# A router's way between token-major and expert-major: TensorE transposes against VectorE 32x32 transposes and a DRAM copy

## The chip, the cores and the metric

One core of a Trainium2 chip runs the whole kernel. The metric is the device time of one execution in microseconds; the figure quoted for a kernel is the median of its runs. Engines are named as in the profile: PE is TensorE's matmul, PEld its weight load, DVE is VectorE, ACT is ScalarE, POOL is GpSimd, SP is the sync engine, which here only issues DMAs.

## What is computed

Four conditional layers are added to a residual stream x of shape (8, 256, 1024), all in float32. Cut to what matters:

```python
# L0: dense layer plus a mixture of 8 low-rank experts, top 2 by logits
logits = x @ Wr.T + 5 * one_hot(language_id, 8)        # (8, 256, 8)
topw, topi = top_k(logits, 2)
gates = sum(one_hot(topi) * softmax(topw))             # (8, 256, 8)
h = einsum('btd,erd->bter', x, A)                      # rank 16 for each expert
x = x + x @ W.T + 2 * einsum('bter,bte,eor->bto', h, gates, B)
# L1: dense, bias, and a per-batch signed mask
x = x + x @ W1.T + b + coeff[b] * (x @ (2 * mask[b] - 1))
# L2: one dense matrix per batch, chosen by an id;  L3: rank 16, chosen by the same id
x = x + x @ w2[id[b]].T
x = x + (x @ B3[id[b]].T) @ A3[id[b]].T
```

The change touches only how `logits` and `gates` are brought from one layout to another.

## The kernel before, in words

Activations are held feature-major: 128 features on the partitions, tokens along the free dimension. Two batches make a pair of 512 tokens, and two pairs make a half `g` (0 or 1). A half goes through L0, and then each of its two pairs through L1, L2 and L3. Every large product is made of three float32r matmuls, from a rounded high part and a low part of each operand. ACT makes the high parts (`highs`, line 285), DVE the low parts by subtraction (`lows`, line 291). The high parts have five buffers and the low parts four, so an engine that prepares operands can be only about two slots ahead of PE.

L0 of a half runs in 16 **slots** (`l0_slot`, line 816). It uses seven products of a Strassen scheme over quadrants of W (named A) and of x (named B); differences such as S1, S4, T1, T3 are made in place, partly by accumulating DMAs from the POOL queue (`add`, line 699). The work around a product is written out by hand: `l0_works` (line 690) lists for each slot what DVE, ACT, POOL and SP are given before the product, in list order, after that slot's high and low parts; a negative slot number means before them. `l0_mids` (line 777) lists what PE is given in the middle of a slot's product or, for a negative number, after it. Each engine and each DMA queue works through what it was given in order.

**The router.** For a pair p, `logits(p)` (line 301) makes eight matmuls of 32 weight columns (8 of them used) by 512 tokens. They are spread over the four 32-column groups of the array, two contraction blocks on each, so PSUM then holds four partial sums on partition groups 0, 32, 64 and 96. ACT copies this bank to SBUF (`leave`, line 310). `by_token(p)` (line 315) makes four TensorE transposes, so that tokens lie on the partitions. `router` (line 323) adds the four partial sums with a DVE reduction, adds the language bias and finds the two best experts in 12 more small DVE operations. `weigh` (line 358) takes an exponential on ACT and makes the gates on DVE. `expand(p)` (line 378) repeats each gate 16 times, once for each rank, with a DVE copy. `gates_by_rank(p)` (line 387) makes four more TensorE transposes and an ACT copy into `gts[p]`: 128 partitions (expert, rank) by 512 tokens. `gate(p)` (line 405) multiplies this by the experts' products `phs[p]` on DVE; `split_gates` (line 398) makes the high part on ACT (`ghi`) and the low part on DVE (`glo`). PE uses these in `lora` (line 647): at the end of slot 5 for the first pair p0 of a half, in slot 9 for the second pair p1, in slots 13 and 15 again.

In half 0, p0 is pair 1 and p1 is pair 0. The logits of p0 are made in `head` (line 848), those of p1 in the middle of slot 3. In half 1 both pairs' logits are made near the end of the previous pair's L2 (line 932), and `router` and `weigh` run once for both (line 999).

**SP's queue.** At the start SP issues all loads that half 0 of L0 needs (lines 1066 to 1087), ending with the two halves of quadrant A22. What follows in its queue is `load_unit` (line 214), which is called from slot 7 on and loads a mask block (line 225), and for some units a block of W1 (line 222). The pool for these blocks has nine buffers, and the eight quadrants of W fill eight of them. Stores of results go through the same queue (line 474).

Of the kernel before, what the change touches and what calls it, by code (L numbers as in the profile page):

```python
# [8 lines left out]
F32 = mybir.dt.float32  # L9
# [3 lines left out]
ALU = mybir.AluOpType  # L13
AX = mybir.AxisListType

P = 128
NB = 8
T = 256
N = 2 * T
K = 8  # L20
E = 8
R = 16
# [12 lines left out]
def kernel(ctx: ExitStack, tc: tile.TileContext, x, lang, coeff, ids,  # L35
# [14 lines left out]
    nc = tc.nc  # L50
# [8 lines left out]
    gp = ctx.enter_context(tc.tile_pool(name="g", bufs=1))  # L59
    ps = ctx.enter_context(tc.tile_pool(name="ps", bufs=2, space=PS))  # L60
    aux = ctx.enter_context(tc.tile_pool(name="aux", bufs=1, space=PS))

    f32 = lambda ap: ap.bitcast(F32)
    mm = nc.tensor.matmul
# [2 lines left out]
    def tt(o, a, b, op):  # L67
        nc.vector.tensor_tensor(o, a, b, op)  # L68

    def bank(n, name):  # L70
        return aux.tile([P, N], F32, tag=f"ax{n}", name=name)
# [30 lines left out]
    c_sb = cst.tile([P, NB], F32, name="c_sb")  # L102
    ids_raw = cst.tile([1, NB], I32, name="ids_raw")
    b1_sb = cst.tile([P, K], F32, name="b1_sb")
    bias = cst.tile([P, NB, E], F32, name="bias")
    c2 = cst.tile([P, NB], F32, name="c2")
    negc = cst.tile([P, NB], F32, name="negc")
    ids_sb = cst.tile([1, NB], I32, name="ids_sb")
# [8 lines left out]
    def constants():  # L117

        lang_f = cst.tile([P, NB], F32, name="lang_f")
        nc.vector.tensor_scalar(lang_f, lang_i, -1.0, float(E), ALU.mult, ALU.add)  # L120
        tt(bias, rev.to_broadcast([P, NB, E]),
           lang_f.rearrange("p (b o) -> p b o", o=1).to_broadcast([P, NB, E]), ALU.is_equal)
        nc.vector.tensor_scalar(bias, bias, 5.0, None, ALU.mult)
        nc.vector.tensor_scalar(c2, c_sb, 2.0, None, ALU.mult)
        nc.vector.tensor_scalar(negc, c_sb, -1.0, None, ALU.mult)

        neg = cst.tile([1, NB], F32, name="neg")
        idf = cst.tile([1, NB], F32, name="idf")
        nc.vector.tensor_scalar(neg, ids_raw, 0.0, float(E), ALU.is_lt, ALU.mult)
        tt(idf, ids_raw, neg, ALU.add)  # L130
        nc.vector.tensor_scalar(ids_sb, idf, 0.0, float(E - 1), ALU.max, ALU.min)
# [164 lines left out]
        ready["lo"] = max(ready["lo"], n + 1)  # L296


    lgs, pts = {}, {}

    def logits(p):


        g, j = p // 2, 1 - p % 2
        pl = bank(j, f"pl{p}")
        for k in range(K):
            c = 32 * (k % 4)
            mm(pl[c:c + 32, :], wrs[:, k, :], X[g][:, j, k, :], start=(k < 4), stop=(k >= 4))  # L308

        def leave():  # L310
            lgs[p] = gp.tile([P, N], F32, tag="lg", name=f"lg{p}", bufs=3)
            copy(lgs[p], pl)
        return leave

    def by_token(p):
        pts[p] = bank(1 - p % 2, f"pt{p}")
        lg = lgs.pop(p)
        for n in range(4):
            nc.tensor.transpose(pts[p][:, n * P:(n + 1) * P], lg[:, n * P:(n + 1) * P], ident)  # L319

    gxs, routed = {}, {}

    def router(pairs):
        n4 = 4 * len(pairs)
        t = lambda nm, w: gp.tile([P, n4, w], F32, tag=nm, name=nm)
        lv = t("lv", E)
        for i, p in enumerate(pairs):
            quarters = pts.pop(p).rearrange("p (n g e) -> p n e g", n=4, g=4)[:, :, :E, :]
            nc.vector.tensor_reduce(
                lv[:, 4 * i:4 * i + 4].rearrange("p n (e o) -> p n e o", o=1), quarters, AX.X,  # L330
                ALU.add)
        b0, nb = 2 * pairs[0], 2 * len(pairs)
        lv4 = lv.rearrange("p (b h) e -> p b h e", h=2)
        tt(lv4, lv4, bias[:, b0:b0 + nb].rearrange("p b (o e) -> p b o e", o=1)
           .to_broadcast([P, nb, 2, E]), ALU.add)
        revb = rev.to_broadcast([P, n4, E])

        def top(v, nm):
            mx = t(f"mx{nm}", 1)
            nc.vector.tensor_reduce(mx, v, AX.X, ALU.max)  # L340
            eq = t(f"eq{nm}", E)
            tt(eq, v, mx.to_broadcast([P, n4, E]), ALU.is_equal)
            tt(eq, eq, revb, ALU.mult)
            fi = t(f"fi{nm}", 1)
            nc.vector.tensor_reduce(fi, eq, AX.X, ALU.max)
            oh = t(f"oh{nm}", E)
            tt(oh, revb, fi.to_broadcast([P, n4, E]), ALU.is_equal)
            return mx, oh

        m1, oh1 = top(lv, "1")  # L350
        rest = t("rest", E)
        nc.vector.scalar_tensor_tensor(rest, oh1, -3.0e38, lv, ALU.mult, ALU.add)
        m2, oh2 = top(rest, "2")
        d = t("d", 1)
        tt(d, m2, m1, ALU.subtract)
        routed[tuple(pairs)] = d, oh1, oh2

    def weigh(pairs):

        n4 = 4 * len(pairs)  # L360
        t = lambda nm, w: gp.tile([P, n4, w], F32, tag=nm, name=nm)
        d, oh1, oh2 = routed.pop(tuple(pairs))
        ex = t("ex", 1)
        nc.scalar.activation(ex, d, AF.Exp)

        den = t("den", 1)
        nc.vector.tensor_scalar(den, ex, 1.0, 0.5, ALU.add, ALU.mult)
        wt1 = t("wt1", 1)
        nc.vector.reciprocal(wt1, den)
        wt2 = t("wt2", 1)  # L370
        tt(wt2, wt1, ex, ALU.mult)
        tt(oh1, oh1, wt1.to_broadcast([P, n4, E]), ALU.mult)
        tt(oh2, oh2, wt2.to_broadcast([P, n4, E]), ALU.mult)
        tt(oh1, oh1, oh2, ALU.add)
        for i, p in enumerate(pairs):
            gxs[p] = oh1[:, 4 * i:4 * i + 4, :]

    def expand(p):

        gx = gp.tile([P, 4 * E, R], F32, tag="lg", name=f"gx{p}", bufs=3)  # L380
        nc.vector.tensor_copy(gx, gxs[p].rearrange("p n (e o) -> p (n e) o", o=1)
                              .to_broadcast([P, 4 * E, R]))
        gxs[p] = gx

    gts, gates, phs = {}, {}, {}

    def gates_by_rank(p):

        pg = bank(1 - p % 2, f"pg{p}")
        gx = gxs.pop(p)  # L390
        for n in range(4):
            nc.tensor.transpose(pg[:, n * P:(n + 1) * P],  # L392
                                gx[:, n * E:(n + 1) * E, :].rearrange("p e r -> p (e r)"),
                                ident)
        gts[p] = gp.tile([P, N], F32, tag="lg", name=f"gt{p}", bufs=3)
        copy(gts[p], pg)

    def split_gates(key, gt):
        hi = gp.tile([P, N], FR, tag="ghi", name="ghi", bufs=2)
        lo = gp.tile([P, N], FR, tag="glo", name="glo", bufs=2)  # L400
        copy(hi, gt)
        tt(lo, gt, f32(hi), ALU.subtract)
        gates[key] = hi, lo
# [286 lines left out]
    def l0_works(g):  # L690
# [5 lines left out]
        def at(s, *fs):  # L696
            w.setdefault(s, []).extend(fs)
# [24 lines left out]
        def both(f, *args):  # L722
            return [lambda h=h: f(h, *args) for h in range(2)]
# [8 lines left out]
        if g == 0:  # L732
            at(1, constants, *both(s1_add))
            at(2, *both(less, "T1", 1, 0), lambda: router([p0]))
            at(3, lambda: weigh([p0]), lambda: expand(p0), lb_parts, *subs("S2", "A11", "S1"))
            at(4, *both(s4_add), lambda: gate(p0))
            at(5, lambda: router([p1]))
            at(6, lambda: weigh([p1]), lambda: expand(p1))
        else:
            at(0, *both(s1_add), *both(less, "T1", 1, 0))  # L740
            at(2, lambda: expand(p0))
            at(3, *subs("S2", "A11", "S1"))
            at(4, *both(s4_add), lambda: gate(p0))
            at(5, lambda: expand(p1))
        at(-5 if g else 4, lambda: split_gates(p0, gts[p0]))
        at(4, *both(less, "T3", 1, 1))
        t2 = subs("T2", "T1", "B22")
        at(7, t2[0], *both(s3_add))
# [28 lines left out]
    def l0_mids(g):  # L777


        p0, p1 = pair_of(g, 0), pair_of(g, 1)  # L780
        if g == 0:
            return {3: lambda: [logits(p1)(), gates_by_rank(p0)], -3: lambda: by_token(p1),
                    7: lambda: gates_by_rank(p1)}
        mids = {0: lambda: proj_pair(1, 0), 1: lambda: rank_pair(1, 1, (0, 1)),
                2: lambda: gates_by_rank(p0), 6: lambda: gates_by_rank(p1)}
        mids.update({s: lambda: fill(2) for s in (3, 4, 5, 7)})
        return mids

# [59 lines left out]
    def head():  # L848

        chain(0, 0)  # L850
        for s in range(2):
# [10 lines left out]
            for k in range(2):  # L862
# [16 lines left out]
                low(w, k, m * P, m * P + P)  # L879
                la_parts(0, m, m + 1)  # L880
                if m == 3:
                    leave = logits(1)
                    highs(4)
                    leave()
                product(s, 0, [k], start=(s == 0), order=order)
                experts(0, 1, v, m, k)
            folded.update((v, w))
        by_token(1)


    pos_tile = {}
# [7 lines left out]
    def main(n):  # L899
# [16 lines left out]
        else:  # L916
# [12 lines left out]
                    mid = [lambda: fill(2)]  # L929
            if q == 1:  # L930
                if u == 13:
                    mid = [lambda: [leave() for leave in [logits(p) for p in (2, 3)]]]
                if u == 14:
                    mid = [lambda: [by_token(p) for p in (2, 3)]]
            if q == 3:
                b = NB - 1
                if u == 9:
# [249 lines left out]
```

## Time and profile before

| | |
|---|---|
| median of 3 runs (600.59 to 601.76) | 600.69 us |
| the profiled execution | 600.37 us |
| its span in the profile | 598.5 us |
| PE busy | 590.9 us, 99% of the span |
| DVE busy / ACT busy / POOL busy | 472.7 / 386.5 / 135.7 us |
| moved by DMA | 130.22 MB, mean 218 GB/s |
| logits: matmul records | 64, of 592 ns each (median) |
| transposes: matmul records | 32, of 272 ns each (median) |

[...] successive matmuls overlap; so the price of one is read from the distance between starts, not from its duration. Each float32 matmul of the logits appears as two records, each transpose and each float32r matmul as one.

### The profile page before, as it was taken

How to read it: one execution, taken by the hardware profiler on the slowest of the kernel's cores; microseconds unless marked ns; L12 is line 12 of the kernel's file. 1: busy time of each engine (PE TensorE's matmuls, PEld its weight loads, DVE VectorE, ACT ScalarE, POOL GpSimd, SP SyncE). 2: the span in 40 equal slices, each digit the busy share in tenths (PEclk: the TensorE clock that was granted, in tenths of full speed). 3: DMA queues.
4: the chain of work that ended last, by engine and by line, in shares of the span. 5: the costliest groups of instructions: out<-in, count | busy, mean ns of one | idle time of the engine just before them, and what ended most of it. 6: DMA issues, size and time to landing. Idle time of an engine off the chain costs nothing.

```text
span 598.5 us, 8945 instructions
## 1 busy us (share of the span) xinstructions
PE 590.9 (99%) x3240; PEld 500.1 (84%) x3240; DVE 472.7 (79%) x561; ACT 386.5 (65%) x460; POOL 135.7 (23%) x178
## 2 busy tenths in 40 slices
PE   9999999999999999999999999999999999999995
PEld 7777888888888888888778888888888888888884
DVE  6678788899789998585856796789968999966863
ACT  5667566687669886544553874568866888764431
POOL 2322260113131143122110234100433110421000
PEclk9999999999999999999999999999999999999999
DMA  8987894567685777499940799836767576745704
GB/s 295 334 208 162 199 238 129 202 251 258 222 271 185 290 271 251 156 367 346 266 70 34 157 247 235 243 106 211 291 201 258 205 292 231 298 158 184 240 1 140
DMA packets 39533, 130.22 MB, mean 218 GB/s; under 512 B 4802, under 2 KB 6466, under 8 KB 38722
## 3 DMA queue, kind: packets, MB, share of 16 engines
q1 hardware_dynamic: 34594, 112.36, 53.1%
q0 software_dynamic: 4608, 16.78, 15.2%
q10 hardware_dynamic: 288, 0.52, 0.3%
q8 instruction: 25, 0.41, 0.3%
q14 instruction: 18, 0.15, 0.1%
HBM read 121.25 MB, written 8.39 MB: 217 GB/s over the span
## 4 chain that ended last, share of the span: by engine, by line
PE 97%; ACT 1%; issue 0%; DVE 0%; DVEq 0%; POOL 0%; POOLq 0%; ACTq 0%
PE po L614 59%; PE mm L614 29%; PE pl L308 1%; PE pf L470 1%; PE pb L442 1%; PE ph L645 1%; PE ph L643 1%; PE ph L644 1%; PE warm L1052 1%; ACT whi L288 1%; PE pb L493 0%; PE po L561 0%; ACT x L719 0%; PE pg L392 0%; PE pt L319 0%
## 5 line engine op out<-in xcount | busy, mean ns | idle before, releaser
L614 PE MATMUL po<-hl,whi 128*128 128x512 f32 x1016 | 244.8, 391 | 0.0
L614 PEld LDWEIGHTS po<-hl,whi 128*128 128x128 f32 x1016 | 186.0, 188 | 35.6
L68 DVE TENSOR_TENSOR wlo<-raw,whi 128x1024 fp32r<-128x1024 f32 x128 | 159.8, 1256 | 4.0 <-issue 2.0
L288 ACT CAST whi<-raw 128x1024 fp32r<-128x1024 f32 x128 | 133.7, 1048 | 18.1 <-PE mm L614 8.3
L614 PEld LDWEIGHTS po<-hl,wlo 128*128 128x128 f32 x1016 | 130.4, 191 | 7.2 <-issue 2.5
L614 PE MATMUL po<-hl,wlo 128*128 128x256 f32 x1016 | 133.4, 283 | 0.0
L614 PE MATMUL mm<-whi,whi 128*128 128x512 f32 x224 | 88.5, 395 | 0.1
L614 PE MATMUL mm<-wlo,whi 128*128 128x512 f32 x224 | 87.7, 391 | 0.0
L235 POOL TENSOR_TENSOR raw<-raw,ident 128x128 f32<-128x128 f32 x72 | 59.2, 827 | 120.8 <-DMA raw<-in_w 95.9
L257 ACT ACTIVATE raw<-raw,negc,c 128x1024 f32<-128x1024 int32 x64 | 79.6, 1243 | 4.2 <-DMA raw<-in_mask 4.0
L614 PE MATMUL mm<-whi,wlo 128*128 128x512 f32 x224 | 70.6, 390 | 0.0
L68 DVE TENSOR_TENSOR raw<-raw,w 128x1024 f32<-128x1024 f32 x56 | 69.3, 1238 | 1.2 <-issue 1.2
L235 POOL TENSOR_TENSOR w<-w,ident 128x128 f32<-128x128 f32 x28 | 32.4, 1157 | 164.2 <-DMA w<-in_w 110.7
L68 DVE TENSOR_TENSOR wlo<-x,whi 128x1024 fp32r<-128x1024 f32 (+1 forms) x38 | 44.3, 1175 | 15.6 <-issue 6.8
L587 ACT COPY c<-po 128x512 f32<-128x512 f32 (+1 forms) x34 | 18.8, 552 | 50.6 <-PE po L614 50.6
L614 PEld LDWEIGHTS mm<-whi,whi 128*128 128x128 f32 x224 | 42.3, 189 | 10.7 <-issue 1.3
L288 ACT CAST whi<-A 128x1024 fp32r<-128x1024 f32 x26 | 27.3, 1051 | 36.0 <-PE mm L614 24.0
L614 PEld LDWEIGHTS mm<-whi,wlo 128*128 128x128 f32 x224 | 42.2, 188 | 9.0
L614 PEld LDWEIGHTS mm<-wlo,whi 128*128 128x128 f32 x224 | 42.2, 188 | 8.5
L590 ACT ACTIVATE sum<-po,b_sb 128x512 f32<-128x512 f32 (+1 forms) x36 | 23.1, 640 | 30.0 <-PE po L614 30.0
L288 ACT CAST whi<-x 128x1024 fp32r<-128x1024 f32 x34 | 35.3, 1049 | 10.8 <-PE mm L614 10.7
L68 DVE TENSOR_TENSOR wlo<-A,whi 128x1024 fp32r<-128x1024 f32 (+3 forms) x37 | 35.7, 980 | 7.8 <-DMA A<-in_w 5.0
(129 smaller groups left out, 509.1 us busy)
## 6 DMA issues: line engine op xcount, KB each, us to landing
raw<-in_mask SPq DMA_DIRECT2D x64, 512.0 KB, 5.5
raw<-in_w SPq DMA_DIRECT2D x64, 512.0 KB, 4.5
w<-in_w SPq DMA_DIRECT2D x28, 512.0 KB, 3.4
out<-c SPq DMA_DIRECT2D x29, 256.0 KB, 3.9
A<-in_w SPq DMA_DIRECT2D x14, 512.0 KB, 8.8
x<-in_x SPq DMA_DIRECT2D x6, 1024.0 KB, 7.8
A<-in_w POOLq DMA_DIRECT2D x12, 512.0 KB, 8.7
x<-in_x POOLq DMA_DIRECT2D x12, 512.0 KB, 8.7
```

Of the source, the lines that this page charges most:

```text
L68: nc.vector.tensor_tensor(o, a, b, op)
L235: (eng or nc.gpsimd).tensor_tensor(t, t, ident, ALU.add)
L257: nc.scalar.activation(f32(raws[n]), raws[n], AF.Identity, bias=negc[:, b:b + 1], scale=c2[:, b:b + 1])
L288: copy(prep_hi(i), flat(source(i)))
L308: mm(pl[c:c + 32, :], wrs[:, k, :], X[g][:, j, k, :], start=(k < 4), stop=(k >= 4))
L442: mm(pb[c:c + 32, j * T:(j + 1) * T], l3b[b][:, k, :], xts[b][:, k, :], start=(k < 4), stop=(k >= 4))
L470: mm(po[:, i * T:(i + 1) * T], at[:, (m + i) * P:(m + i + 1) * P], rt, start=True, stop=True)
L587: copy(xs, po[:, :, T:])
L590: nc.scalar.activation(xs, po[:, :, T:], AF.Identity, bias=b1c)
L614: mm(*args, skip_group_check=True, **kw)
L643: mm(phs[p], hi, v[0][:, kk], start=(k == 0), stop=False)
L644: mm(phs[p], hi, v[1][:, kk], start=False, stop=False)
```

## The change

- `logits(p)` no longer spreads the contraction over the four column groups. Column group g of the array takes quarter g of the tokens, 128 of them, and accumulates all eight contraction blocks: 32 matmuls of 128 tokens in the place of 8 of 512. PSUM then holds complete logits: expert on the partition within a group of 32, token along 128 columns. The ACT copy out of PSUM is gone.
- `by_token` is gone. `router` makes one DVE transpose per pair, which transposes each 32x32 block of the 128x128 PSUM region, and the DVE reduction over partial sums is gone. The bias tile is laid out for the new place of the tokens, with one more small DVE operation in `constants`.
- `weigh` writes the gates into the transposed tile and makes a second DVE transpose per pair back to (expert, token).
- `expand(p)` is now four SP DMAs per pair to a DRAM scratch, from 8 partitions each, each row of 128 tokens repeated 16 times: 512 bytes a piece, 64 KB a DMA. `gates_by_rank(p)` is one SP DMA of 256 KB back to `gts[p]`. Its four TensorE transposes and its ACT copy are gone.
- In half 0 the read back of p0 is given to SP in slot 3 right after the writes. `router` of p1 moves from slot 5 to slot 4, behind `split_gates` of p0, and `weigh` and `expand` of p1 from slot 6 to slot 5; its read back is in slot 6. In half 1 both `expand` move to slot 0, the read backs to slots 3 and 6.

```diff
     def logits(p):
-        g, j = p // 2, 1 - p % 2
-        pl = bank(j, f"pl{p}")
+        a, j = p // 2, 1 - p % 2
+        pls[p] = bank(j, f"pl{p}")
         for k in range(K):
-            c = 32 * (k % 4)
-            mm(pl[c:c + 32, :], wrs[:, k, :], X[g][:, j, k, :], start=(k < 4), stop=(k >= 4))
-
-        def leave():
-            lgs[p] = gp.tile([P, N], F32, tag="lg", name=f"lg{p}", bufs=3)
-            copy(lgs[p], pl)
-        return leave
-
-    def by_token(p):
-        pts[p] = bank(1 - p % 2, f"pt{p}")
-        lg = lgs.pop(p)
-        for n in range(4):
-            nc.tensor.transpose(pts[p][:, n * P:(n + 1) * P], lg[:, n * P:(n + 1) * P], ident)
+            for g in range(4):
+                mm(pls[p][32 * g:32 * g + 32, :P], wrs[:, k, :],
+                   X[a][:, j, k, g * P:(g + 1) * P], start=(k == 0), stop=(k == K - 1))
...
     def router(pairs):
+        lt = t("lt", 32)
+        for i, p in enumerate(pairs):
+            nc.vector.transpose(flat(lt[:, 4 * i:4 * i + 4]), pls.pop(p)[:, :P])
...
     def weigh(pairs):
-        tt(oh1, oh1, oh2, ALU.add)
+        tt(lt[:, :, :E], oh1, oh2, ALU.add)
         for i, p in enumerate(pairs):
-            gxs[p] = oh1[:, 4 * i:4 * i + 4, :]
+            gxs[p] = gp.tile([P, P], F32, tag=f"gx{i}", name=f"gx{p}")
+            nc.vector.transpose(gxs[p], flat(lt[:, 4 * i:4 * i + 4]))
...
     def expand(p):
-        gx = gp.tile([P, 4 * E, R], F32, tag="lg", name=f"gx{p}", bufs=3)
-        nc.vector.tensor_copy(gx, gxs[p].rearrange("p n (e o) -> p (n e) o", o=1)
-                              .to_broadcast([P, 4 * E, R]))
-        gxs[p] = gx
+        by_rank[p] = dram.tile([E, R, N], F32, tag=f"ranks{p}", name=f"ranks{p}")
+        gx = gxs.pop(p)
+        for g in range(4):
+            src = gx[32 * g:32 * g + E].rearrange("e (o t) -> e o t", o=1)
+            nc.sync.dma_start(by_rank[p][:, :, g * P:(g + 1) * P],
+                              src.to_broadcast([E, R, P]))

     def gates_by_rank(p):
-        pg = bank(1 - p % 2, f"pg{p}")
-        gx = gxs.pop(p)
-        for n in range(4):
-            nc.tensor.transpose(pg[:, n * P:(n + 1) * P],
-                                gx[:, n * E:(n + 1) * E, :].rearrange("p e r -> p (e r)"),
-                                ident)
         gts[p] = gp.tile([P, N], F32, tag="lg", name=f"gt{p}", bufs=3)
-        copy(gts[p], pg)
+        nc.sync.dma_start(gts[p], by_rank.pop(p).rearrange("e r c -> (e r) c"))
...
             at(3, lambda: weigh([p0]), lambda: expand(p0), lb_parts, *subs("S2", "A11", "S1"))
             at(4, *both(s4_add), lambda: gate(p0))
-            at(5, lambda: router([p1]))
-            at(6, lambda: weigh([p1]), lambda: expand(p1))
         else:
             at(0, *both(s1_add), *both(less, "T1", 1, 0))
-            at(2, lambda: expand(p0))
             at(3, *subs("S2", "A11", "S1"))
             at(4, *both(s4_add), lambda: gate(p0))
-            at(5, lambda: expand(p1))
         at(-5 if g else 4, lambda: split_gates(p0, gts[p0]))
+        if g == 0:
+            at(4, lambda: router([p1]))
+            at(5, lambda: weigh([p1]), lambda: expand(p1))
+        else:
+            at(0, lambda: expand(p0), lambda: expand(p1))
+        at(3, lambda: gates_by_rank(p0))
+        at(6, lambda: gates_by_rank(p1))
         at(4, *both(less, "T3", 1, 1))
```

More of the change, by code (lines that the diff above doesn't have):

```diff
@@ L61 @@
     aux = ctx.enter_context(tc.tile_pool(name="aux", bufs=1, space=PS))
+    dram = ctx.enter_context(tc.tile_pool(name="dram", bufs=1, space=bass.MemoryType.DRAM))
     f32 = lambda ap: ap.bitcast(F32)
@@ L104 @@
     b1_sb = cst.tile([P, K], F32, name="b1_sb")
-    bias = cst.tile([P, NB, E], F32, name="bias")
+    bias = cst.tile([P, NB // 2, E], F32, name="bias")
     c2 = cst.tile([P, NB], F32, name="c2")
@@ L120, in constants @@
         nc.vector.tensor_scalar(lang_f, lang_i, -1.0, float(E), ALU.mult, ALU.add)
-        tt(bias, rev.to_broadcast([P, NB, E]),
-           lang_f.rearrange("p (b o) -> p b o", o=1).to_broadcast([P, NB, E]), ALU.is_equal)
+        for b in range(2):
+            r = slice(64 * b, 64 * b + 64)
+            tt(bias[r], rev[r].to_broadcast([64, NB // 2, E]),
+               lang_f[r].rearrange("p (q b o) -> p b q o", b=2, o=1)[:, b]
+               .to_broadcast([64, NB // 2, E]), ALU.is_equal)
         nc.vector.tensor_scalar(bias, bias, 5.0, None, ALU.mult)
@@ L296, in lows @@
         ready["lo"] = max(ready["lo"], n + 1)
-    lgs, pts = {}, {}
+    pls = {}
     def logits(p):
-        g, j = p // 2, 1 - p % 2
-        pl = bank(j, f"pl{p}")
+        a, j = p // 2, 1 - p % 2
+        pls[p] = bank(j, f"pl{p}")
         for k in range(K):
-            c = 32 * (k % 4)
-            mm(pl[c:c + 32, :], wrs[:, k, :], X[g][:, j, k, :], start=(k < 4), stop=(k >= 4))
-        def leave():
-            lgs[p] = gp.tile([P, N], F32, tag="lg", name=f"lg{p}", bufs=3)
-            copy(lgs[p], pl)
-        return leave
-    def by_token(p):
-        pts[p] = bank(1 - p % 2, f"pt{p}")
-        lg = lgs.pop(p)
-        for n in range(4):
-            nc.tensor.transpose(pts[p][:, n * P:(n + 1) * P], lg[:, n * P:(n + 1) * P], ident)
+            for g in range(4):
+                mm(pls[p][32 * g:32 * g + 32, :P], wrs[:, k, :],
+                   X[a][:, j, k, g * P:(g + 1) * P], start=(k == 0), stop=(k == K - 1))
     gxs, routed = {}, {}
@@ L325, in router @@
         t = lambda nm, w: gp.tile([P, n4, w], F32, tag=nm, name=nm)
+        lt = t("lt", 32)
+        for i, p in enumerate(pairs):
+            nc.vector.transpose(flat(lt[:, 4 * i:4 * i + 4]), pls.pop(p)[:, :P])
         lv = t("lv", E)
[L327 to L335, printed above, removed]
+        np = len(pairs)
+        tt(lv.rearrange("p (q n) e -> p q n e", q=np),
+           lt.rearrange("p (q n) e -> p q n e", q=np)[:, :, :, :E],
+           bias[:, pairs[0]:pairs[0] + np].rearrange("p q (o e) -> p q o e", o=1)
+           .to_broadcast([P, np, 4, E]), ALU.add)
         revb = rev.to_broadcast([P, n4, E])
@@ L355, in router @@
         tt(d, m2, m1, ALU.subtract)
-        routed[tuple(pairs)] = d, oh1, oh2
+        routed[tuple(pairs)] = lt, d, oh1, oh2
     def weigh(pairs):
@@ L361, in weigh @@
         t = lambda nm, w: gp.tile([P, n4, w], F32, tag=nm, name=nm)
-        d, oh1, oh2 = routed.pop(tuple(pairs))
+        lt, d, oh1, oh2 = routed.pop(tuple(pairs))
         ex = t("ex", 1)
@@ L373, in weigh @@
         tt(oh2, oh2, wt2.to_broadcast([P, n4, E]), ALU.mult)
-        tt(oh1, oh1, oh2, ALU.add)
+        tt(lt[:, :, :E], oh1, oh2, ALU.add)
         for i, p in enumerate(pairs):
-            gxs[p] = oh1[:, 4 * i:4 * i + 4, :]
+            gxs[p] = gp.tile([P, P], F32, tag=f"gx{i}", name=f"gx{p}")
+            nc.vector.transpose(gxs[p], flat(lt[:, 4 * i:4 * i + 4]))
+    gts, gates, phs, by_rank = {}, {}, {}, {}
     def expand(p):
-        gx = gp.tile([P, 4 * E, R], F32, tag="lg", name=f"gx{p}", bufs=3)
-        nc.vector.tensor_copy(gx, gxs[p].rearrange("p n (e o) -> p (n e) o", o=1)
-                              .to_broadcast([P, 4 * E, R]))
-        gxs[p] = gx
-    gts, gates, phs = {}, {}, {}
-    def gates_by_rank(p):
-        pg = bank(1 - p % 2, f"pg{p}")
-        gx = gxs.pop(p)
-        for n in range(4):
-            nc.tensor.transpose(pg[:, n * P:(n + 1) * P],
-                                gx[:, n * E:(n + 1) * E, :].rearrange("p e r -> p (e r)"),
-                                ident)
+        by_rank[p] = dram.tile([E, R, N], F32, tag=f"ranks{p}", name=f"ranks{p}")
[4 more added lines that the diff above has]
+                              src.to_broadcast([E, R, P]))
+    def gates_by_rank(p):
         gts[p] = gp.tile([P, N], F32, tag="lg", name=f"gt{p}", bufs=3)
-        copy(gts[p], pg)
+        nc.sync.dma_start(gts[p], by_rank.pop(p).rearrange("e r c -> (e r) c"))
     def split_gates(key, gt):
@@ L781, in l0_mids @@
         if g == 0:
[L782 to L785, printed above, removed]
+            return {3: lambda: logits(p1)}
+        mids = {0: lambda: proj_pair(1, 0), 1: lambda: rank_pair(1, 1, (0, 1))}
         mids.update({s: lambda: fill(2) for s in (3, 4, 5, 7)})
@@ L881, in head @@
                 if m == 3:
-                    leave = logits(1)
+                    logits(1)
                     highs(4)
-                    leave()
                 product(s, 0, [k], start=(s == 0), order=order)
@@ L887, in head @@
             folded.update((v, w))
-        by_token(1)
     pos_tile = {}
@@ L931, in main @@
                 if u == 13:
-                    mid = [lambda: [leave() for leave in [logits(p) for p in (2, 3)]]]
-                if u == 14:
-                    mid = [lambda: [by_token(p) for p in (2, 3)]]
+                    mid = [lambda: [logits(p) for p in (2, 3)]]
             if q == 3:
```

## The prediction

> **What bounds the kernel now.** I read the page's busy times and chain of waits first, then PE's timeline around the logits and transposes, then the chain in order of time, then the DMA share by stretch.
>
> ```profile
> PE 590.9 (99%) x3240; PEld 500.1 (84%) x3240; DVE 472.7 (79%) x561; ACT 386.5 (65%) x460; POOL 135.7 (23%) x178
> ...
> PE 97%; ACT 1%; issue 0%; DVE 0%; DVEq 0%; POOL 0%; POOLq 0%; ACTq 0%
> ```
>
> PE sets the end: what is taken off its stream is gained, if nothing then keeps it waiting. The exception is one stretch of half 0, where the chain in order of time leaves PE:
>
> ```profile
> 38.15 0.41 ACT whi L288
> 38.56 0.55 issue
> 39.11 1.04 ACT whi L288
> 40.15 0.96 ACT A L713 x2
> ...
> 41.95 0.61 ACT ghi L401
> 42.56 1.91 ACT x L719 x2
> 44.47 1.89 ACT whi L288 x2
> ```
>
> From PE's end of slot 3 to its start of slot 6 (46.86) ACT is just in time: two high parts, two copies for S4, the gates of p0, two negations for T3, two high parts. PE loses only about 0.3 us here (distances of 459 and 335 ns at 46.86 and 47.32 where 227 is usual). Whatever delays the gates of p0 delays this row. DVE's timeline of the same stretch:
>
> ```profile
> 40.38 0.68 DVE L68 TENSOR_TENSOR gt<-ph,gt 128x512 f32<-128x512 f32 x1
> 42.60 0.69 DVE L68 TENSOR_TENSOR glo<-gt,ghi 128x512 fp32r<-128x512 f32 x1 [1.53 <-ACT ghi L401]
> ```
>
> So `gts` of p0 is wanted by 40.4 and has 0.9 us to spare (it ends at 41.06, ACT takes it at 41.95). Third, the DMA: share and rate by stretch, then the mask load that SP issues at 19.5, right behind the initial loads, and its time to landing:
>
> ```profile
> 24.00:32.00 8.00, 8.00 (x37) 6.60 (x36) 7.49 (x24) 5.80 (x8) 1.75 (x2) 1.00 1.05 280
> 32.00:40.00 8.00, 8.00 (x48) 5.30 (x47) 5.91 (x7) 3.22 (x5) 0.00 (x0) 1.00 1.04 273
> ```
>
> ```profile
> L225 SPq DMA_DIRECT2D raw<-in_mask x2: 328/458/587, 19.5 to 55.6; - x2
> ...
> DMA to landing us min/median/max: 3.3/12.6/21.9
> ```
>
> The second number from the right is the DMA share: full until 40 us. A load issued at 19.5 lands 21.9 us later, at 41.4. SP's queue is that far behind.
>
> **What the Trainium skill says.** (1) "DMA: Bandwidth & Descriptors", section "Queues, rings and completion order": each DMA engine takes a ring's descriptors in order and goes round robin between queues packet by packet. The trace agrees: from 24 to 40 us SP's and POOL's queues move 33 to 36 packets each per us, 4 KB of SP's taking 159 to 173 ns and 4 KB of POOL's accumulating ones 327. (2) Same page, section on why a DMA raises its semaphore by 16: the slowest dimension sets the number of engines, so a source of 8 partitions runs on 8. No DMA here has that shape. (3) "TensorE: Matmul & The Clock Gate", Part 1: an idle window of about 3.4 us halves PE's clock. The trace has the cold clock only at the start and after the last matmul.
>
> **The change part by part.** The sum is against the profiled execution, 600.37 us (span 598.5 and 1.9 around it), which is 0.3 below the median of 600.69.
>
> *Transposes removed.* Four of them stand so in PE's timeline:
>
> ```profile
> 318.17 0.62 PE L614 MATMUL mm<-whi,wlo 128*128 128x512 f32 x2
> 318.63 0.60 PE L392 MATMUL pg<-ident,gx 128*128 128x128 f32 x4
> 318.99 0.48 PE L614 MATMUL mm<-whi,whi 128*128 128x512 f32 x1
> 319.30 0.39 PE L614 MATMUL mm<-wlo,whi 128*128 128x512 f32 x1
> ```
>
> 318.63 to 319.30 is 0.67 us, of which one ordinary matmul is 0.23: 0.45 for four. The eight beginning at 293.6 cost 0.89. In all eight groups: 3.5 us, of which 1.3 before PE's slot 4 products are done (p0's two groups and p1's first) and 2.25 after it.
>
> *Logits by quarters.*
>
> ```profile
> 16.25 1.92 PE L308 MATMUL pl<-x,wrs 128*32 128x512 f32 x16
> 18.10 0.50 PE L614 MATMUL mm<-whi,whi 128*128 128x512 f32 x1
> ...
> 302.42 2.06 PE L442 MATMUL pb<-c,b 128*32 128x256 f32 x32
> 304.41 0.50 PE L614 MATMUL mm<-whi,whi 128*128 128x512 f32 x1
> ```
>
> Four records run side by side on the four column groups: every 430 ns at 512 tokens, every 216 at 256. So a token costs 0.836 ns and a group 2.7 ns; at 128 tokens 109 ns. 64 records are 16 groups, 1.75 us beside 1.72 before: 0.1 us for all pairs. The lower bound is zero, since as many tokens stream. The upper one: the weight load (110 ns) no longer fits beside 107 ns of streaming, 217 a group, 1.7 us more per pair. I take 0.1, since a transpose's load of 138 ns fits beside 108 ns. The same skill page, "Wait — 56ns, not 53.3ns?", puts the least distance of matmuls at 25 ns: 64 are 1.6 us (estimate), no bound.
>
> *ACT.* Eight copies of 586 ns go, 4.7 us. They lie in waits for PE (3.00 us before 35.22, 1.79 before 38.15): no gain, ACT restarts when PE frees a high buffer.
>
> *DVE.* Off: reductions (two of 0.28 and two together 0.48) and four copies of 0.42, 2.7 us. On: eight transposes and one bias operation. No transpose of DVE is in the trace; the skill ("VectorE: DVE Perf Modes", "The three transpose paths") gives 311 ns for 128x128 in bf16; I take 0.3, bounds 0.2 and 0.6. Sum about zero, hidden under PE.
>
> *Round trip of p0 (slot 3).* This is the large term. Before, the gx copy ends at 32.6; the transposed gates are there at about 32.0 (PE 0.55 earlier at slot 2). SP is idle and issues four writes by 33.5. But they stand behind both A22 loads: the first lands at 35.0 (issue 18.30, 16.7 to landing), the second, by the landing records, ring by ring from 35.1 to 38.8. The mask, now behind the gates, no longer stands ahead. From about 36.5, on the slowest ring 38.4, 64 packets of 512 bytes per ring (4 DMAs, 128 each, 8 rings) go out. The records give 46 ns for 1 KB and 82 for 2 KB, so 26 each (estimate), and up to three times that if eight rings reading eight partitions hinder each other (an allowance, no row shows it); about 7 packets of POOL's at 327 come between until 40. Landed between 41 and 44. Only then does SP issue the read. A 256 KB transfer in quiet takes:
>
> ```profile
> out<-c SPq DMA_DIRECT2D x4, 256.0 KB, 3.0
> ```
>
> 3.0, plus up to 8 x 0.33 when it alternates with POOL's S4 accumulations, which start about 42.5. `gts` lands at L = 43.5 to 49.5; I take 47.
>
> *What waits.* DVE's gate(p0) blocks DVE until L; 0.7 for it and 0.65 for ghi: ghi at L + 1.4. Behind it on ACT: T3, then slot 5's high parts. Behind it on DVE: glo (0.65), now router(p1), moved ahead of slot 5's low parts (46.58 to 49.55 before: 3.0), then wlo of x and of A (1.15 each). PE's slot 6 wants the latter 0.9 us after its start: effective start L + 1.4 + 0.65 + 3.0 + 2.3 - 0.9, with latencies L + 6.5. Before it was 47.2. PE itself would come at 45.8. With L = 47: 53.5, 6.3 later. PE is full afterwards, so nothing is won back except the 2.25 - 0.1 of later transposes: +4.15.
>
> *Clock.* PE stands from 43.0 (lora) to 48.4. By the skill's window it may go cold: most of the slow work hides in the next wait; 0.6, bounds 0 and 2.
>
> *Round trip of p1, and SP's queue.* Written about 57, read about 64, wanted by gate(p1) at 60.2 + 6.3: nothing, at worst 2. Behind it stands load_unit: mask 0 moves from 19.5 to about 62 and is wanted at 61.4 + 6.3: nothing, at worst 2. The cover is the delay itself.
>
> *Half 1.* Writes from about 302, wanted at 331.2; DMA share there is 0.26 (300 to 330). Hidden 25 us deep.
>
> Sum: 600.37 + 6.3 - 2.15 + 0.6 = 605.1.
>
> **The rivals.**
>
> 1. *The round trip is in time* (faster). In quiet it takes 32.0 + 1.3 + 3.0 + 3.0 = 39.3, before the deadline of 40.4. Then only router(p1) ahead of the low parts matters: slot 6 at 46.6, total 600.37 - 0.6 - 2.15 = 597.6. The net is L - 42.85, so it is faster from L below 42.85. For it: the last A22 rings may not be among the eight, and POOL's last packets are few. Against: the second A22 lands at 38.8 and both legs follow it. 0.20.
> 2. *Logits limited by weight loads*: half 1's two pairs add 3.4 in full, half 0's hide in the stall: 608.5. For it: four times the loads. Against: the transposes' spacing. 0.07.
> 3. *The two cancel*: L near 43, about 600.4 to 601.5. 0.10.
>
> **How the numbers follow.** Late gates 0.63, time 605, own range 601.7 (L = 43.5 with 0.6 for the clock) to 609.5 (L = 49.5 and the worst of one other term). Differences over 0.2% (1.2 us) are what a measurement of this kernel can tell. The range takes in part of rival 1 and all but the top of rival 2: 598 to 609.5. Faster is rival 1's 0.20; same 0.08, most of the third rival; the rest slower 0.72.
>
> **What would show it.** Late gates: DVE's gt<-ph,gt in slot 4 waits 5 to 9 us for the DMA, ACT's ghi follows, PE shows two holes (before lora and before slot 6), and everything later is shifted by a constant less 2.2. The write lands after A22. If logits take over 2.2 us per pair, rival 2. If PE has no hole near 43 us and gt starts by 40.4, I am wrong and it is rival 1.

## The result and the profile after

The changed kernel takes **606.58 us** (median of 6 runs, 606.07 to 609.88) beside 600.74 for the kernel before in the same session: ratio **1.0099, interval 1.0084 to 1.0115**. Slower, by 5.8 us; 605.0 was forecast. The profiled execution took 607.11 us (span 605.3) against 600.37 (598.5).

The page: the busy times and the shares of the chain of waits.

```profile
PE 590.0 (97%) x3400; PEld 503.5 (83%) x3400; DVE 473.1 (78%) x562; ACT 382.5 (63%) x452; POOL 131.4 (22%) x178
...
PE 86%; DMA 7%; DVE 3%; SPq 1%; issue 1%; ACT 1%; DVEq 0%; ACTq 0%
```

PE's busy time is hardly changed (590.9 before), but PE is 86% of the chain instead of 97%, and 7% is DMA, which was not in it. Of these 7%, p0's round trip is 2.2%; the rest are loads, most of them before 24.6 us and one near 290, through which the chain runs now. The round trip in the chain in order of time (start, us, what):

```profile
32.08 0.82 SPq L379
...
34.36 7.54 DMA ranks<-gx
42.06 6.11 DMA gt<-ranks
48.19 0.70 DVE gt L69
...
49.65 68.30 PE mm L603 x288
```

For 14 us the chain that ended last runs through the write of p0's gates to DRAM and their read back. SP's timeline has both round trips of half 0 (p0, then p1):

```profile
32.08 2.94 SPq L379 DMA_DIRECT2D ranks<-gx  x4
42.06 0.34 SPq L385 DMA_DIRECT2D gt<-ranks  x1
56.89 3.62 SPq L379 DMA_DIRECT2D ranks<-gx  x4
63.77 0.32 SPq L385 DMA_DIRECT2D gt<-ranks  x1
```

Each read is issued when its writes are landed: 10.0 and 6.9 us after the first issue. DVE's timeline, with the idle time ahead and what ended it in brackets; the gates that began at 40.38 before begin 7.8 later:

```profile
48.19 0.69 DVE L69 TENSOR_TENSOR gt<-ph,gt 128x512 f32<-128x512 f32 x1 [8.57 <-DMA gt<-ranks]
49.63 0.69 DVE L69 TENSOR_TENSOR glo<-gt,ghi 128x512 fp32r<-128x512 f32 x1 [0.74 <-ACT ghi L390]
...
54.35 1.22 DVE L69 TENSOR_TENSOR wlo<-A,whi 128x1024 fp32r<-128x1024 f32 x1
```

ACT's timeline shows the row that follows on the gates: their high part, T3's two negations, slot 5's two high parts, and the copies of C11, which free the PSUM tiles that slot 6 writes:

```profile
48.98 0.62 ACT L390 CAST ghi<-gt 128x512 fp32r<-128x512 f32 x1 [6.89 <-DVE gt L69]
49.50 2.00 ACT L708 ACTIVATE x<-x 128x1024 f32<-128x1024 f32 x2
51.41 1.03 ACT L292 CAST whi<-A 128x1024 fp32r<-128x1024 f32 x1
52.34 1.04 ACT L292 CAST whi<-x 128x1024 fp32r<-128x1024 f32 x1
...
53.51 0.99 ACT L757 COPY c<-mm 128x1024 f32<-128x1024 f32 x1
```

PE's timeline: the hole before lora, lora at half clock (records 427 ns apart instead of 227), slot 6 right behind it at 54.83 instead of 47.32.

```profile
42.72 0.39 PE L634 MATMUL ph<-whi,laglo 128*128 128x512 f32 x1
49.65 1.22 PE L603 MATMUL mm<-ghi,lb 128*128 128x512 f32 x2 [6.54 <-ACT ghi L390]
50.66 0.63 PE L603 MATMUL mm<-glo,lb 128*128 128x512 f32 x1
...
54.83 0.39 PE L603 MATMUL mm<-whi,whi 128*128 128x512 f32 x1
```

Set beside each other, the starts of the same matmuls in the two traces give an **offset** (after minus before), which shows where time is lost and won: -1.3 at 40.4, +5.4 at lora, +7.5 at slot 6, +6.9 after p1's group, +6.1 at 300 (the two groups of half 1's logits gone), then +7.4 again inside the pb matmuls of half 1, +6.5 at the end. The logits by quarters and that late loss, in PE's timeline:

```profile
32.77 1.96 PE L311 MATMUL pl<-x,wrs 128*32 128x128 f32 x64
34.66 0.50 PE L603 MATMUL mm<-whi,whi 128*128 128x512 f32 x1
```

```profile
308.46 1.06 PE L431 MATMUL pb<-c,b 128*32 128x256 f32 x14
310.45 1.48 PE L431 MATMUL pb<-c,b 128*32 128x256 f32 x18 [0.93 <-DVE c L69]
```

```profile
308.19 0.51 DVE L369 STREAM_TRANSPOSE gx<-lt 128x128 f32<-128x128 f32 x2
...
309.72 0.68 DVE L69 TENSOR_TENSOR c<-po,c 128x512 f32<-128x512 f32 x1
```

A pair's logits take 1.89 us (1.85 before). The pb matmuls (the product with B3 for the last pair of half 0) stop in the middle for the last L2 result. DVE makes it (`c<-po`) behind half 1's router, which has become 0.5 us longer: its transposes for the way out stand there too. In the kernel before, the work for the way out came later, in slots 2 to 6, and the pb matmuls run through.

### The profile page after: what moved, and what is told of

Its sections match the earlier page's. It is cut to its first block, busy times and chain, and to the rows that moved or that the text cites. A ratio compares the mean times of both kernels' runs of the same rounds, so it can differ in the third digit from the quotient of the medians.

```text
span 605.3 us, 9283 instructions
## 1 busy us (share of the span) xinstructions
PE 590.0 (97%) x3400; PEld 503.5 (83%) x3400; DVE 473.1 (78%) x562; ACT 382.5 (63%) x452; POOL 131.4 (22%) x178
## 4 chain that ended last, share of the span: by engine, by line
PE 86%; DMA 7%; DVE 3%; SPq 1%; issue 1%; ACT 1%; DVEq 0%; ACTq 0%
PE po L603 55%; PE mm L603 25%; DMA a3raw<-in_a 2%; DMA x<-in_x 1%; DMA ranks<-gx 1%; DMA c<-in_la 1%; PE pf L459 1%; DVE wlo L69 1%; DMA gt<-ranks 1%; DMA A<-in_w 1%; PE pb L431 1%; DVE c L69 1%; PE ph L632 1%; PE ph L633 1%; PE ph L634 1%
## 5 line engine op out<-in xcount | busy, mean ns | idle before, releaser
L239 POOL TENSOR_TENSOR w<-w,ident 128x128 f32<-128x128 f32 x28 | 26.2, 936 | 165.0 <-DMA w<-in_w 117.8
L69 DVE TENSOR_TENSOR c<-mm,c 128x1024 f32<-128x1024 f32 x20 | 24.5, 1223 | 21.7 <-PE mm L603 21.7
```

The lines of the kernel that those rows point to most:

```text
L239: (eng or nc.gpsimd).tensor_tensor(t, t, ident, ALU.add)
```

## The experiments

The theory: p0's round trip is late and takes the place of the transposes. Open were which part of it is slow, whether the clock adds to it, and where the rest of PE's saving went. Every ratio is to the kernel before on the same chip.

### The way to DRAM and back

**A22's loads behind p0's round trip.** Undoes the write's place in SP's order.

```
-    for h in range(2):
-        load_w0(0, "A22", h)
...
         at(3, lambda: gates_by_rank(p0))
+        if g == 0:
+            at(3, lambda: [load_w0(0, "A22", h) for h in range(2)])
```

> The two loads of A22 are issued after p0's read back, so nothing of SP's stands ahead of p0's writes. Theory of late gates by SP's ring: the writes begin about 33 and not 36, alternate with POOL's packets until 38, have landed about 40 (42.1 in the changed kernel); gates are there at 44 to 46 and not 48.1; PE's hole before lora shrinks from 6.7 us to 3 to 5; total 602.5 to 604.5. If POOL's traffic alone sets the pace of the small packets: landed at 41.5 to 42, total 606. If the loss is not in the round trip at all (logits, DVE transposes, router order): 606.6 unchanged.

602.26, ratio 1.0035 (1.0023 to 1.0046). SP's timeline, then DVE's:

```profile
32.20 5.46 SPq L379 DMA_DIRECT2D ranks<-gx  x4
40.58 0.34 SPq L385 DMA_DIRECT2D gt<-ranks  x1
```

```profile
43.33 0.69 DVE L69 TENSOR_TENSOR gt<-ph,gt 128x512 f32<-128x512 f32 x1 [3.59 <-DMA gt<-ranks]
```

With nothing ahead in SP's queue the writes still take 8.4 us. Only 1.5 us of the 4.9 gained on the gates is the write leg; the rest is the read, 2.7 instead of 6.1, now over before the data of the S4 accumulations, which the DMA records show from 44.

**p0's four writes from ACT's queue**, A22 staying where it was (p0 of half 0 is pair 1).

```
-            nc.sync.dma_start(by_rank[p][:, :, g * P:(g + 1) * P],
+            (nc.scalar if p == 1 else nc.sync).dma_start(by_rank[p][:, :, g * P:(g + 1) * P],
```

> p0's four writes go through ACT's DMA queue, everything else as in the changed kernel. If it is the order of SP's ring that holds the writes back: they land about 39.5 instead of 42.1, total about 604. If it is that each packet of 512 bytes takes one turn against a 4 KB packet of each other queue: landed about 41.5, total 606 within 0.5. If the loss is elsewhere: 606.6.

606.93, ratio 1.0106 (1.0089 to 1.0123): no gain. The read is issued at 41.85, 0.2 earlier. So the place behind A22 in the ring is not what holds the writes. Nothing stands ahead of them in ACT's queue, and still their first packet begins at 36.34 by the DMA records, 4.3 us after the first issue, when A22's packets in SP's queue run low.

**S4's copies and accumulations behind p0's gates.** Clears the read's way instead.

```
-            at(4, *both(s4_add), lambda: gate(p0))
+            at(4, lambda: gate(p0))
...
         at(-5 if g else 4, lambda: split_gates(p0, gts[p0]))
+        if g == 0:
+            at(4, *both(s4_add))
```

> S4's copies and accumulating DMAs are given after the gates of p0, so POOL's queue is empty during p0's read back. Theory that the read back alternates with POOL's accumulations: its time from issue falls from 6.0 us to about 3.2, gates at 45.3, PE's hole before lora about 3.8 us, total 603 to 604. If the read back is slow by itself: 6 us again and total 606.6 or more, since S4's copies now stand behind the gates on ACT.

607.31, ratio 1.0111 (1.0094 to 1.0128). The read leg is 2.5 us (41.74 to 44.28), shorter than expected, and the total is not better: a miss. ACT's timeline and PE's show why.

```profile
45.07 0.62 ACT L390 CAST ghi<-gt 128x512 fp32r<-128x512 f32 x1 [5.64 <-DVE gt L69]
45.59 1.99 ACT L702 COPY A<-A 128x1024 f32<-128x1024 f32 x2
47.49 2.00 ACT L708 ACTIVATE x<-x 128x1024 f32<-128x1024 f32 x2
...
51.38 1.90 ACT L758 COPY c<-mm 128x1024 f32<-128x1024 f32 x2
```

```profile
52.42 0.79 PE L603 MATMUL mm<-whi,whi 128*128 128x512 f32 x1 [3.36 <-ACT c L758]
53.01 0.63 PE L603 MATMUL mm<-wlo,whi 128*128 128x512 f32 x1
```

S4's two copies now stand ahead of C11's on ACT. lora starts at 45.74 at full clock, but slot 6 waits for its PSUM tiles until 52.42 and then runs at half clock for 6 us. Gates 3.9 us earlier brought slot 6 only 2.4 forward, and the clock took that.

**Short writes**: the copying over 16 ranks moves to the read, so the writes are 32 packets of 512 bytes instead of 512.

```
-        by_rank[p] = dram.tile([E, R, N], F32, tag=f"ranks{p}", name=f"ranks{p}")
+        by_rank[p] = dram.tile([E, N], F32, tag=f"ranks{p}", name=f"ranks{p}")
...
+            nc.sync.dma_start(by_rank[p][:, g * P:(g + 1) * P], gx[32 * g:32 * g + E])
...
+        src = by_rank.pop(p).rearrange("e (o c) -> e o c", o=1)
+        nc.sync.dma_start(gts[p], src.to_broadcast([E, R, N]))
```

> The changed kernel with the copying over the 16 ranks moved from the write to the read: each of the four writes puts 8 rows of 512 bytes into DRAM (32 packets in all, before 512), the read takes each row 16 times. The order in the rings stays: behind A22. If the number of packets, each taking one turn beside POOL's queue, is what makes the write leg long, the write is landed by 39.5 to 40 (A22 ends at 38.4, then one or two turns), the read is issued near 40 and meets little of the S4 accumulations: gates near 43, as in the run with A22 behind, 602.3. If a latency of the write that does not depend on the number of packets holds it, the read is issued at 41.5 or later, the gates come at 46 to 48 and it is 605.5 to 606.5.

604.01, ratio 1.0082 (1.0058 to 1.0105). The read is issued at 38.9 instead of 42.06 and the gates begin at 42.66, as the first theory has it: in this execution fewer packets are worth 3 us. The total lies between the two expectations. (This median is 2.4 over the profiled run, 601.59, the fastest of the six; they scatter from there to 607.83.)

**Short writes and A22 behind.**

> Both: short writes (32 packets), and A22's loads behind p0's round trip in SP's order. If turns beside POOL's queue are the cost: the writes are issued by 33.5 and landed by 36, the read (8 packets per ring, each a turn of 0.33, and 2 us around) lands at 40.5 to 41.5; PE has no hole before lora beyond 0.5 us, slot 6 starts near 47.5 and it is 598 to 599. If the first packets come only at 36 again, whatever their number, the read is issued at 38 to 39.5, the gates come at 41.5 to 42.5 and it is 599.5 to 601.

601.18, ratio 1.0014 (1.0007 to 1.0020), just above the second expectation. SP's timeline, then PE at slot 6:

```profile
31.48 1.31 SPq L378 DMA_DIRECT2D ranks<-gx  x4
37.65 0.70 SPq L384 DMA_DIRECT2D gt<-ranks  x1
```

```profile
47.80 0.50 PE L602 MATMUL mm<-whi,whi 128*128 128x512 f32 x1 [1.59 <-ACT c L758]
```

Four DMAs of 4 KB with nothing ahead of them take 6.2 us. The read, which now does the copying, takes 3.8 (2.7 with A22 behind and plain reading). PE's hole before lora is only 0.43 us, but slot 6 waits 1.59 us for ACT's copies of C11, as it does with A22 behind and with short writes alone. The DMA records of these traces, counted by queue (packets begun in each us), show when they move:

```
us                            33   34   35   36   37   38   39   40
changed kernel, SP's queue    43   36   26   33   29   26  148  275
   "            POOL's        45   36   43   49   51   45   39    7
A22 behind,     SP's           0    0    2  144  143  163   88    4
   "            POOL's        61   56   55   27    7    2    0    0
short + behind, SP's           0    0   54   10    0    0   65  105
   "            POOL's        66   53   47   17    2    0    0    0
```

(SP's row holds A22's packets too, up to 38 in the changed kernel, and in the last run the read from 39.) In the changed kernel the 512-byte packets (27 ns alone) get at most one turn for each of POOL's (327 ns) until POOL's queue runs out at 40, and then go at 275 per us. With A22 away they do not even get that: none moves before POOL's queue begins to empty, for 32 packets as for 512. (Then 512 of them go at about 140 per us and not 275; why is open.)

### The clock

**30 unread matmuls of the identity ahead of p0's lora**, so that PE has no idle window.

```
                 part = lora(p0, lb_half(0))
+                if g == 0:
+                    hold = bank(0, "hold")
+                    for n in range(30):
+                        mm(hold[:, :P], ident, ident, start=True, stop=True)
```

> Thirty matmuls on the identity, which nobody reads, stand before lora of p0 in half 0 and fill most of PE's hole. Lora's matmuls are then 227 ns apart and not 427, so lora is done 2.3 us earlier. Theory that the router of p1 ahead of the low parts is late at the same moment: slot 6 must wait for the low part of A (done at 55.6), total 606.3, at most 0.5 below the changed kernel. If the cold clock is a loss of its own: 604.3.

606.21, ratio 1.0091 (1.0075 to 1.0108). lora runs at full clock (0.998 over the run), and PE then waits 1.29 us for ACT's copies of C11: slot 6 starts at 53.47 instead of 54.83. Most of that is not the clock: p0's gates happen to come 1.1 us earlier in this execution (ACT's ghi at 47.88 instead of 48.98). From ghi to slot 6 it takes 5.59 us instead of 5.85, so the clock cost about 0.3. The total is 0.4 us less, inside both intervals: the cold clock was nearly free, since ACT and DVE were almost as late as PE.

### Where the saved transposes went

**The way in alone**: logits by quarters and VectorE's transpose; the way out and its schedule as before.

```
-        tt(lt[:, :, :E], oh1, oh2, ALU.add)
+        tt(oh1, oh1, oh2, ALU.add)
...
+        copy(gts[p].rearrange("p (g n t) -> p n g t", g=4, n=4),
+             pg.rearrange("p (n g t) -> p n g t", n=4, g=4))
```

> The way in alone: logits by quarters and VectorE's transpose of them stay; the way out is that of before (copy of 128x512 on VectorE, four TensorE transposes per pair, a copy on ScalarE, and the schedule of before). If the loss of the change is all in the DRAM round trip of p0, this is before less four groups of transposes and plus 0.1 for the logits: 600.4 - 4 x 0.45 + 0.1 = 598.7, with up to 599.6 if half 1's share is swallowed again. PE then starts slot 6 at about 45.8 to 46.9 us, without a hole before lora. If instead the logits by quarters or VectorE's transposes cost something that the traces do not show, it is 601 or more.

600.34, ratio 1.0001 (0.9993 to 1.0009). The loss is in the way out, but four groups of transposes less on PE (1.8 us) gain nothing: a miss of both expectations. The offset to the kernel before is -0.73 at 40.4, -0.25 at slot 6, -1.10 ahead of the pb matmuls, -0.19 after them. PE at slot 6:

```profile
47.07 0.50 PE L607 MATMUL mm<-whi,whi 128*128 128x512 f32 x1 [0.56 <-ACT c L758]
```

PE is there earlier and waits for ACT's copies of C11. In the kernel before PE and ACT arrived there together, so what PE saves ahead of it is lost. The pb matmuls take back another 0.9.

**p0 by TensorE, the other three pairs by DRAM**, schedule as in the changed kernel.

```
+        if p == 1:
+            pg = bank(1 - p % 2, f"pg{p}")
...
+            return
         gts[p] = gp.tile([P, N], F32, tag="lg", name=f"gt{p}", bufs=3)
```

> The changed kernel with one round trip taken out: p0 of half 0 goes out by TensorE's four transposes and ScalarE's copy, p1 and all of half 1 by DRAM, and the router of p1 stays ahead of slot 5's low parts. If p0's round trip is the whole loss, seven of eight groups of transposes are gained: 600.4 - 7 x 0.45 + 0.1 = 597.3, up to 598.6 with half 1's gain swallowed; slot 6 starts near 46.9. If the router of p1 ahead of the low parts, p1's round trip or half 1's round trips cost something too, slot 6 is late by 1 to 3 us without any wait for DMA, and it is 599.5 to 601.5.

599.50, ratio 0.9989 (0.9982 to 0.9995). One round trip of four is the whole loss: without it the change gains 0.9 us, and slot 6 is not late (46.78). But seven groups (3.1 us) were to give more. Half 1's pb matmuls swallow 1.4 (offset -1.66 ahead of them, -0.24 after):

```profile
302.76 1.48 PE L452 MATMUL pb<-c,b 128*32 128x256 f32 x18 [0.94 <-DVE c L69]
```

That is 0.5 more than with the way in alone, where DVE makes no transposes for the way out (0.51 us) ahead of the last L2 result.

**The same, and half 1's router behind the last L2 result.** Only the two transposes stay; the other 5 us of DVE go to slot 1.

```
-                router([2, 3])
-                weigh([2, 3])
+                take([2, 3])
...
-            at(0, lambda: expand(p0), lambda: expand(p1))
+            at(1, lambda: router([2, 3]), lambda: weigh([2, 3]))
+            at(1, lambda: expand(p0), lambda: expand(p1))
```

> The kernel with p0 by TensorE and the rest by DRAM, and in half 1 only VectorE's transposes of the logits stay before the last L2 result; the rest of the router of half 1 (about 5 us of VectorE) and its writes go to slot 1 of half 1. If the router in front of the last L2 result is what swallowed PE's gain of half 1 (PE came to the pb matmuls 1.56 us ahead of the kernel before and left them 0.34 ahead), the 1.2 us stay: 599.5 - 1.2 = 598.3. If something else is late next there (an input's load, ScalarE's high parts), or the router in slot 1 delays slot 1's low parts or its writes miss slot 4, it is 599.3 or more.

597.99, ratio 0.9956 (0.9943 to 0.9968). The pb matmuls run through:

```profile
301.89 1.93 PE L458 MATMUL pb<-c,b 128*32 128x256 f32 x32
303.76 0.50 PE L630 MATMUL mm<-whi,whi 128*128 128x512 f32 x1
```

So DVE's router ahead of the last L2 result swallowed PE's gain. (In the profiled execution, 598.86 and the slowest of five, p1's gates are late too: the offset goes from -0.98 to +0.34 at slot 8. p1's round trip in this schedule is just in time, and not in every run.)

### Can the DRAM trip be hidden?

**Slot 6's row freed**, with short writes and A22 behind: T3's negations to slot 7, p1's router behind slot 5's low parts.

```
-            at(4, lambda: router([p1]))
-            at(5, lambda: weigh([p1]), lambda: expand(p1))
+            at(5, lambda: router([p1]))
+            at(6, lambda: weigh([p1]), lambda: expand(p1))
...
-        at(4, *both(less, "T3", 1, 1))
+        at(4 if g else 7, *both(less, "T3", 1, 1))
```

> Short writes and A22 behind p0's round trip (601.2 so far), and the row in front of slot 6 freed: T3's two negations on ScalarE (1.9 us, wanted only by slot 12) go to slot 7, and the router of p1 goes behind slot 5's low parts as in the kernel before. Gates of p0 still near 41.4. If slot 6 is late only by what stands ahead of the copies of C11 on ScalarE and of A's low part on VectorE, it starts at 46.2 to 46.6 instead of 47.8, and the whole is 1.2 to 1.6 less: 599.6 to 600.0. If lora itself, late with the gates, sets slot 6, it stays at 47.3 or later and 600.7 to 601.2. T3's loads no longer run when p1's gates are written: if the writes of 32 packets waited for POOL's queue, p1's are landed 2.5 to 3 us after their issue, before 5.4; if not, 5 us again.

601.29, ratio 1.0020 (1.0010 to 1.0029). Slot 6 starts at 46.42, as expected, and the total does not follow. (T3 and the router are moved together, so this run does not tell their shares apart.) SP's timeline for p1, then DVE's:

```profile
52.79 1.31 SPq L378 DMA_DIRECT2D ranks<-gx  x4
55.09 0.60 SPq L384 DMA_DIRECT2D gt<-ranks  x1
```

```profile
62.84 0.69 DVE L69 TENSOR_TENSOR gt<-ph,gt 128x512 f32<-128x512 f32 x1 [4.09 <-DMA gt<-ranks]
```

The same four writes are landed after 2.3 us when POOL's queue is empty (5.6 with T3's loads in it, in the run with short writes and A22 behind): for p1's writes the wait for POOL's queue is confirmed. p0's were issued while POOL's queue was full in every run that has them. But T3's loads, moved, now meet p1's read, which takes 7.7 us; the offset goes from -1.3 to +0.4 at slot 8.

**The same with half 1's router in slot 1.**

> Both together: short writes, A22 behind, slot 6's row freed, and half 1's router in slot 1. If both causes are right and independent, 599.6 to 600.0 less 1.2: 598.4 to 598.8. If only one is, 599.6 to 600.1.

600.27, ratio 1.0002 (0.9990 to 1.0014), just above the second expectation: 1.0 us better than the last, as half 1's share should be, with p1's gates still late.

**The same with T3's negations and loads behind p1's gates (slot 8).**

```
-        at(4 if g else 7, *both(less, "T3", 1, 1))
+        if g:
+            at(4, *both(less, "T3", 1, 1))
...
         at(8, lambda: split_gates(p1, gts[p1]), t2[1])
+        if g == 0:
+            at(8, *both(less, "T3", 1, 1))
```

> The version with short writes, A22 behind, slot 6's row freed and half 1's router in slot 1, and T3's two negations and loads not in slot 7 but behind p1's gates in slot 8, so that they meet neither the write nor the read of p1. If the wait for p1's gates (PE 1.10 us late at slot 8's lora, its offset to the kernel before going from -1.39 to +0.31) is what took back the gain of the freed row, it does not appear: slot 6 at 46.4 to 47.0, offset -0.9 to -1.4 kept through slot 8, then the later transposes of half 0 and 1 count in full: offset about -3 at the end, 597.0 to 597.8. If p1's gates are late all the same (S3's loads in their way), or T3's loads make mask or weight loads late, it is 599 to 600.5.

598.05, ratio **0.9956 (0.9942 to 0.9970)**, 0.25 above the first expectation; offset -2.5 at the end. DVE's timeline:

```profile
42.34 0.69 DVE L69 TENSOR_TENSOR gt<-ph,gt 128x512 f32<-128x512 f32 x1 [2.43 <-DMA gt<-ranks]
...
59.26 0.69 DVE L69 TENSOR_TENSOR gt<-ph,gt 128x512 f32<-128x512 f32 x1
```

p1's gates wait for nothing; p0's are still 2 us after those of before, and cost 0.5 us of PE (offset -1.03 ahead of lora, -0.50 from slot 6 on). With all four pairs by DRAM the change is a gain of 2.7 us once no long wait takes its place; it equals the version that keeps p0 on TensorE, and both beat the kernel before. The five runs no longer scatter either: 597.67 to 598.67, where those with a round trip just late went from 600.23 to 603.79 (p1's) or from 600.76 to 606.09 (A22 behind).

## Why the prediction was right

It named late gates of p0 as the likeliest case, and the case came, with most of its signs: DVE's wait (8.57 us), ACT's ghi behind it, the write landing after A22. Of the two holes of PE only the one before lora came, and what was won back later was half of the forecast. Step by step:

- *Gates at L = 47*: 48.1. The write leg landed in the forecast span (42.0 of 41 to 44), the read took 6.1 where 3.0 and up to 2.6 were counted. Alternation with POOL was right: taken away, the read is 2.5 to 2.7. "They stand behind both A22 loads" was **wrong as the cause**: on ACT's queue the writes are as late. What holds them is the load of the other queues, POOL's above all, by the DMA records; an experiment shows it for p1's writes only. A22 away gives 1.5 us, fewer packets 3.
- *Slot 6 6.3 us later, and 0.6 for the clock*: 7.5. The second hole is missing because lora at half clock takes 5.2 us (49.65 to 54.83) and fills it. With earlier gates, or with PE kept busy, it is there (1.29 to 1.59 us), but those runs put it down to a wait that the prediction did not name: ACT's copies of C11 behind T3. The wait named, for A's low part behind p1's router (54.35 to 55.57), ends at about the same time, so the sum held by luck. The clock fell as expected and cost about 0.3.
- *Less 2.15 later*: the groups are worth their price (offset +7.5 to +6.9, 6.1 by 300, and 0.9 more in half 1), but 1.4 comes back at the pb matmuls. **This is the term that was mis-sized**: net 1.0, not 2.15. "What is taken off its stream is gained, if nothing then keeps it waiting" was applied without asking that of half 1, where DVE is just in time: that takes 0.9. The other 0.5 is DVE's own transposes for the way out, which "Sum about zero, hidden under PE" overlooked: they stand ahead of the last L2 result. The first rival, 597.6, had the same flaw: with p0's trip gone, the kernel took 599.5, and 598.0 only when that row was freed too.
- *Logits*: 0.04 per pair, 0.1 at most: right; the weight loads are no bound. *VectorE's transposes* 0.31 us against 0.3 taken.
- *p1's round trip, mask, half 1's trips: nothing*: right in the changed kernel, under cover of the delay, as said. With the delay gone p1's read became the next wait (62.84 above).

Sum: +7.5 - 0.6 - 0.9 + 1.4 - 0.9 = 6.5, the offset at the end, against 4.75 forecast. The two misses add: 0.6 more up to slot 6, 1.1 less won back.

## What to carry to other kernels

Before a detour through DRAM takes work off the bound engine, find the deadline of its result and the DMA queues that are busy in between; price both legs under that load, not in quiet, and keep replication out of the write. A saving on the bound engine counts only up to the next wait for an engine that was just in time: follow the offset between two traces past each such row. When a transfer or a step is moved out of the way, look at what it meets in its new place.

## What the runs showed of the hardware

- **Small writes under another queue's load.** "DMA: Bandwidth & Descriptors", section "Queues, rings and completion order", in the Trainium skill says that each DMA engine goes round its queues packet by packet. The counts above agree in the changed kernel, but not with A22 away, where small packets issued at about 32 get no turn until POOL's queue begins to empty at 35 to 36: the first packet comes 3.6 us after the issue for 4 KB writes (35.06 after 31.48), 0.8 with POOL's queue empty (p1's, 53.55 after 52.79). p1's do the same: landed after 5.6 us beside POOL's loads, 2.3 without. Why they wait is open, and so is whether their size matters: no run issued a large DMA at that point instead.
- **The clock can halve after less idle time than stated.** "TensorE: Matmul & The Clock Gate", Part 1, puts the idle window at about 3.4 us. The holes of 6.54 and 3.36 us fit. But in the profiled execution with half 1's router in slot 1 and T3 in slot 7, PE waits only 1.91 us before slot 8's lora. The view by stretches of that kernel (busy time of PE, PE's loads, DVE, ACT and POOL, then PE's clock, the DMA share and GB/s):

```profile
64.00:66.00 2.00, 0.43 (x2) 0.39 (x3) 1.83 (x3) 0.62 (x1) 0.00 (x1) 1.00 1.04 266
66.00:68.00 2.00, 2.00 (x8) 1.52 (x7) 2.00 (x3) 0.02 (x1) 0.00 (x0) 0.62 1.09 250
68.00:70.00 2.00, 2.00 (x6) 1.60 (x5) 2.00 (x2) 2.00 (x2) 0.00 (x0) 0.53 1.04 238
```

The clock is near a half for 4 us, while a hole of 2.51 us, with S4 behind p0's gates, left it full. This is one trace, but probably no single event: 7 of that kernel's 14 runs, the profiled one among them, have a mean granted clock of 0.993 or 0.994 and take 600.02 to 603.60 us; the other 7 have 0.995 to 0.998 and take 599.01 to 600.33.
- **VectorE's transpose** of 128x128 in fp32 (32x32 blocks) took 0.31 us, out of PSUM and out of SBUF: the price that "VectorE: DVE Perf Modes" gives for bf16, in "The three transpose paths".
